# Attention of a four-layer network: moments, preparation and settling of a block cut into smaller parts, one part to a round

## The chip, the cores and the metric

The kernel runs on one core of a Trainium2 chip. The metric is the device time of one execution in microseconds (us), as the median of several runs. The engines are named as the profile names them: PE is TensorE (PEld its weight loads), DVE is VectorE, ACT is ScalarE, POOL is GpSimd, SP is SyncE.

## What is computed

The reference has four layers: a deformable convolution, a gated state-space layer, an attention by products of cosines with a feed-forward network and a mixture of experts, and last an additive attention with a second mixture of experts. The change touches the additive attention alone. For each of 4 images, with 4096 tokens of 128 channels, it computes, in float32:

```
v     = layernorm(t)                                    # over the 128 channels
s_ij  = w2 . tanh(v_i W1[:128] + v_j W1[128:] + b1) + b2   # for j before i
out_i = sum_{j<i} exp(s_ij) v_j / (sum_{j<i} exp(s_ij) + tiny)
t     = t + out
```

(The output is a softmax over the earlier tokens; 16 hidden units stand between the two matrices.)

## The kernel before

**What replaces tanh.** With the exponentials F = exp(2 f_i) and G = exp(2 g_j) of the two projections, exp(s_ij) can be written with a few sums of products F x G, their logarithm, and an exponential. The 16 hidden units are folded into three sets of products over 32 or 64 rows. For a tile of 128 keys j and 512 queries i, PE forms three denominators (D, three banks of PSUM) and three numerators (num1, num2); ACT takes Ln of D and Exp of its negative; DVE multiplies by the numerators; POOL adds the three terms to one sum q; and in a later round ACT takes Exp of the negative of q, which gives the weights e. PE then multiplies v by e and adds into acc.

**Blocks and rounds.** A block is one image n and 512 queries, ib = 0 to 7. Its keys are taken 128 at a time, so block ib has 4 ib + 3 rounds (3, 7, 11, ... 31; the last two rounds hold the pieces at the diagonal); 136 rounds an image, 544 in all. `blocks` (L2123) lists them. One round is one call of `step` (L2268), and the order in which `step` issues things is the order on every engine: the class InOrder keeps program order, and each engine works through its queue in that order. In one call, `products` (L2132) issues

- on PE the denominators of this round and the numerators of the round two calls before;
- on ACT one Ln over this round's D (r<-D), one Exp (r<-r) over that and over the q of an earlier round (2048 columns in one instruction when both are whole);
- on DVE two multiplications by numerators (r<-r,num, 1024 and 512 columns), on POOL two additions (r<-r);
- on DVE, for pieces on the diagonal, a multiplication by a triangular mask (r<-r,keep, L2213) right after this round's Exp. It comes four calls after the round whose piece it is, so it falls into rounds 1, 2 and 3 of the next block.

After that, `step` runs the functions of `later`, each holding what it got for one call: first one that only delays, then `weigh` (L2219; acc += v e on PE, and at a block's end the copy aT<-acc on DVE), then `settle` (L2232): four transposes of aT on PE into bank 3 of D, the copy zs<-D, the reciprocal den, a row sum zl, and four additions onto X, all in one call. `LAG = 4 + len(later)` is the number of empty calls at the end, and of the calls after which a block's tiles are free.

**Preparation of the next block.** While a block runs, its successor is prepared by the generator `prepare` (L2088), a part at each `next(ahead)` at the end of `step`. The parts: 0, for an even q, `statistics` (L2070), the moments of eight tiles for two blocks (eight bn_stats, six small DVE instructions, then Ln and Exp of rstd on ACT), and nothing for an odd q; 1, the norm (four v<-X,mean,rstd); 2, four transposes on PE and the copy vT<-D; 3 to 6, one product each with wf or wg (D<-vT) and its exponential on ACT, F, F, G, G, with a maximum on DVE (top) and for G a scaling on POOL in the part after; 7, the last of these. The parts are spread evenly over the block's rounds (`to`, L2290), in block 7 from round 11 on.

**Bank 3.** D has four banks. A round takes banks 0 to 2 (side 0) or 1 to 3 (side 1), so that two rounds can alternate. What `aux()` (L2024) returns, for transposes and the wf and wg products, is bank 3. Therefore a round in which bank 3 is taken, and the round after it, have side 0:

```
taken = held[-1] is not None or any(p in ON_BANK for p in parts)
side = int(last[0] == 0 and not taken and not last[1])
again = side == last[0]
```

`again` says that a round has the same side as the one before, so its denominators have to wait for that round's Ln; then `products` issues the numerators ahead of the denominators on PE, and otherwise the first denominator ahead.

Of the kernel before, what the change touches and what calls it, by code (L numbers as in the profile page):

```python
# [16 lines left out]
P = 128  # L17
# [3 lines left out]
NT = L // P  # L21
# [67 lines left out]
class Kernel:  # L89
# [1903 lines left out]
    def attention(self):  # L1993
# [10 lines left out]
        tc, nc = self.tc, self.nc  # L2004
        T = self.X.rearrange("p (t c) -> p t c", c=P)
        LAST = P - 1
        LIMIT = 4.0e8
        with ExitStack() as outer:
# [7 lines left out]
            with ExitStack() as ctx:  # L2016
# [7 lines left out]
                def aux():  # L2024
                    return D[:, 3, :]
# [24 lines left out]
                def aside(op):  # L2050
                    held_to(op, some(logs[1]) + uses, some(logs[2]))
# [15 lines left out]
                nc = InOrder(tc)  # L2067
                pieces, norm = {}, [None]

                def statistics(t0):  # L2070

                    st = sp.tile([P, 8, 6], F32, name="st")
                    mean = sp.tile([P, 8], F32, name="mean")
                    rstd = sp.tile([P, 8], F32, name="rstd")
                    d = sp.tile([P, 8], F32, name="d")
                    for k in range(8):
                        nc.vector.bn_stats(st[:, k, :], T[:, t0 + k, :])
                    nc.vector.tensor_add(mean, st[:, :, 1], st[:, :, 4])
                    nc.vector.tensor_scalar(mean, mean, 0.5, None, ALU.mult)
                    nc.vector.tensor_sub(d, st[:, :, 1], st[:, :, 4])  # L2080
                    nc.vector.tensor_mul(d, d, d)
                    nc.vector.tensor_add(rstd, st[:, :, 2], st[:, :, 5])
                    nc.vector.scalar_tensor_tensor(rstd, d, 32.0, rstd, ALU.mult, ALU.add)
                    nc.scalar.activation(rstd, rstd, AF.Ln, bias=self.eps5, scale=1.0 / P)
                    nc.scalar.activation(rstd, rstd, AF.Exp, scale=-0.5)
                    norm[0] = mean, rstd

                def prepare(n, q):  # L2088

                    v = vs[q]  # L2090
                    if q % 2 == 0:
                        statistics(n * NT + 4 * q)
                    yield
                    mean, rstd = norm[0]
                    for k in range(4):
                        t = n * NT + 4 * q + k
                        nc.vector.tensor_scalar(v[:, k, 0:LAST], T[:, t, 0:LAST], mean[:, t % 8:t % 8 + 1],
                                                rstd[:, t % 8:t % 8 + 1], ALU.subtract, ALU.mult)
                    yield
                    pd = aux()  # L2100
                    for k in range(4):
                        aside(nc.tensor.transpose(pd[:, k * P:(k + 1) * P], v[:, k, :], self.ident))
                    vT = rp.tile([P, 512], F32, name="vT", bufs=1)
                    uses[:] = [nc.vector.tensor_copy(vT, pd)]
                    wrote[0] = None
                    yield
                    out = {"v": v, "F": [], "G": []}
                    for k, (to, m) in enumerate((("F", wf[0]), ("F", wf[1]), ("G", wg[0]), ("G", wg[1]))):
                        ps = aux()
                        aside(nc.tensor.matmul(ps, m, vT, start=True, stop=True))  # L2110
                        t = bp.tile([P, 512], F32, name=f"{to}{k % 2}" + (f"_{q}" if to == "G" else ""),
                                    bufs=1 if to == "G" else 3)
                        uses[:] = [nc.scalar.activation(t, ps, AF.Exp, scale=2.0)]
                        wrote[0] = t
                        out[to].append(t)
                        yield
                        nc.vector.tensor_reduce(top[:, 8 * n + q, k:k + 1], t, AX.X, ALU.max)
                        if to == "G":
                            nc.gpsimd.tensor_scalar(t, t, cw[k % 2], None, ALU.mult)
                    pieces[n, q] = out  # L2120
                    yield

                def blocks(ib):  # L2123


                    for jt in range(4 * ib + 1):
                        yield [(jt, slice(0, 512), slice(0, 512))]
                    yield [(4 * ib + 1, slice(128, 512), slice(0, 384)),
                           (4 * ib + 3, slice(384, 512), slice(384, 512))]
                    yield [(4 * ib + 2, slice(256, 512), slice(256, 512))]  # L2130
# [101 lines left out]
                def settle(n, ib, aT):  # L2232

                    z = aux()
                    for s in range(4):
                        aside(nc.tensor.transpose(z[:, s * P:(s + 1) * P], aT[:, s * P:(s + 1) * P], self.ident))
                    zs = ep.tile([P, 512], F32, name="zs", bufs=1)
                    uses[:] = [nc.vector.tensor_copy(zs, z)]
                    wrote[0] = None
                    z = zs.rearrange("p (s c) -> p s c", c=P)  # L2240
                    den = sm.tile([P, 4], F32, name="den")
                    nc.vector.tensor_scalar(den, z[:, :, LAST], tiny, None, ALU.add)
                    nc.vector.reciprocal(den, den)
                    zl = sm.tile([P, 4], F32, name="zl")
                    nc.vector.tensor_reduce(zl, z[:, :, 0:LAST], AX.X, ALU.add)
                    nc.vector.tensor_mul(zl, zl, den)
                    t0 = n * NT + 4 * ib
                    for s in range(4):
                        tt = T[:, t0 + s, 0:LAST]
                        nc.vector.scalar_tensor_tensor(tt, z[:, s, 0:LAST], den[:, s:s + 1], tt, ALU.mult, ALU.add)  # L2250
                    tl = T[:, t0:t0 + 4, LAST]
                    nc.vector.tensor_sub(tl, tl, zl)
# [2 lines left out]


                order = [(n, q) for n in range(NB) for q in range(8)]
                for _ in prepare(*order[0]):
                    pass
                later = [lambda *a: a, weigh, settle]  # L2260
                LAG = 4 + len(later)
                waiting, sums = [None, None], [None, None]
                spaces = [rp.tile([P, 4, 512], F32, name="r", bufs=RB) for k in range(2)]
                held = [None] * len(later)
                PARTS, ON_BANK = 8, (2, 3, 4, 5, 6)
                last = [0, False]

                def step(block, parts=()):  # L2268


                    taken = held[-1] is not None or any(p in ON_BANK for p in parts)
                    side = int(last[0] == 0 and not taken and not last[1])
                    again = side == last[0]
                    last[:] = side, taken
                    new_held, new_sum, new = products(block, side, again, waiting.pop(), sums.pop())
                    waiting.insert(0, new_held)
                    sums.insert(0, new_sum)
                    for k in range(len(later)):
                        new, held[k] = (later[k](*held[k]) if held[k] is not None else None), new
                    for _ in parts:  # L2280
                        next(ahead)

                for k, (n, ib) in enumerate(order):
                    ahead, done = (prepare(*order[k + 1]), 0) if k + 1 < len(order) else (None, PARTS)
                    todo = list(blocks(ib))
                    rounds = len(todo)

                    first = 4 + LAG if ib == 7 else 0
                    for r, parts in enumerate(todo):
                        to = -(-PARTS * max(r - first + 1, 0) // (rounds - first))  # L2290
                        step((n, ib, parts, r == rounds - 1), range(done, max(done, to)))
                        done = max(done, to)
                for k in range(LAG):
                    step(None)
                nc = self.nc
# [200 lines left out]
```

## Time and profile before

| | |
|---|---|
| median of 3 runs | 5611.95 us (5593.98 to 5615.91) |
| the profiled execution | 5601.23 us, its span 5599.5 us |
| mean granted PE clock | 0.941 |
| busy over the span | PE 4991.9 (89%), DVE 4016.3 (72%), ACT 3113.9 (56%), POOL 3073.1 (55%) |
| the attention | 3077 to 5218 us of the span, 2141 us |
| r<-D (Ln) of the attention | 544, one a round; 1.44 us over 1536 columns |
| r<-r (Exp) over 2048 columns | 1.91 us |
| moments, settling | 16 and 32 times |
| F and G exponentials | 128, 0.58 us each |

How to read it: the page gives the shares over the whole span, and the attention is only 2141 us of it. Nearly every instruction of the attention is recorded under one line, L82, the helper that keeps the program order; so instructions are found by engine and by the tiles that they write and read (r<-D is one that reads D and writes r). In a timeline the columns are the start and the length in us, engine, line, operation, tiles, shapes and count, and in brackets the idle time ahead of it on its engine and who ended it.

### The profile page before, as it was taken

Reading aid. Unit: us, or ns where it says so; the run is one execution under the profiler, and the core shown is the slowest. Engines: PE = TensorE matmul, PEld = TensorE weight load, DVE = VectorE, ACT = ScalarE, POOL = GpSimd, SP = SyncE. Lnnn points to the kernel's source line nnn. Section 1 sums busy time; section 2 is a strip of 40 time slices with the busy share of each in tenths; the row PEclk is TensorE's granted clock in tenths of the full one; section 3 lists DMA queues with packets and bytes.
Section 4 is the critical chain, followed back from the end, with each engine's and each line's share of the span. In section 5 each row is a group of like instructions: output and inputs, shape, how many; then the busy total and the mean of one; then the engine's idle time right before and its main releaser. Section 6 shows DMA issues by size and latency. Waiting matters only on the chain. (4 is left out here: it accounts for less than half of the span.)

```text
span 5599.5 us, 62830 instructions
## 1 busy us (share of the span) xinstructions
PE 4991.9 (89%) x21718; PEld 2404.9 (43%) x21718; DVE 4016.3 (72%) x7854; ACT 3113.9 (56%) x3785; POOL 3073.1 (55%) x3027
## 2 busy tenths in 40 slices
PE   6898989879999859999887899989998998999887
PEld 3454444335656523333443344434433444344443
DVE  6888988758876578786698565666566666665796
ACT  1122222146655345555431689878978987889431
POOL 0525253314444324454399577666766776667597
PEclk8999999989988779999899899999999999999899
DMA  5545454400000020000000000000000000000001
GB/s 171 126 131 128 124 132 127 98 6 1 16 16 12 27 61 1 1 1 1 6 31 16 16 1 1 1 1 1 1 1 1 1 1 1 1 1 1 5 1 61
DMA packets 66743, 185.21 MB, mean 33 GB/s; under 512 B 13158, under 2 KB 16038, under 8 KB 64744
## 3 DMA queue, kind: packets, MB, share of 16 engines
q1 hardware_dynamic: 55792, 163.68, 9.9%
q0 software_dynamic: 6272, 12.86, 1.4%
q10 hardware_dynamic: 4344, 4.50, 0.3%
q8 instruction: 175, 2.87, 0.2%
q14 instruction: 160, 1.31, 0.1%
HBM read 131.63 MB, written 49.36 MB: 32 GB/s over the span
## 5 line engine op out<-in xcount | busy, mean ns | idle before, releaser
L82 POOL TENSOR_TENSOR r<-r 128x512 f32<-128x512 f32 (+1 forms) x1088 | 1349.0, 1241 | 661.9 <-DVE r L82 597.0
L82 DVE TENSOR_TENSOR r<-r,num 128x1024 f32<-128x1024 f32 (+1 forms) x1088 | 970.4, 927 | 564.3 <-PE num L82 514.1
L82 PE MATMUL D<-F,G 32*128 32x512 f32 (+3 forms) x4608 | 1218.8, 589 | 1.9 <-POOL G L82 1.0
L82 PE MATMUL num<-F,G 32*128 32x512 f32 (+3 forms) x4608 | 1084.5, 604 | 105.4 <-DVE r L82 101.6
L82 ACT ACTIVATE r<-r 128x2048 f32<-128x2048 f32 (+4 forms) x610 | 1018.3, 1679 | 49.2 <-POOL r L82 3.4
L82 ACT ACTIVATE r<-D 128x1536 f32<-128x1536 f32 (+1 forms) x544 | 764.2, 1405 | 206.1 <-PE D L82 174.2
L82 PE MATMUL acc<-pr,ident 128*128 128x512 f32 x1600 | 749.4, 619 | 79.4 <-DVE pr L82 79.4
L82 PEld LDWEIGHTS D<-F,G 32*128 32x128 f32 x4608 | 507.2, 189 | 327.4 <-issue 217.2
L82 PE MATMUL acc<-r,v 128*128 128x512 f32 (+3 forms) x1152 | 606.4, 614 | 3.1 <-DVE aT L82 3.1
L82 PEld LDWEIGHTS num<-F,G 32*128 32x128 f32 x4608 | 394.4, 187 | 410.9 <-DVE r L82 239.5
L1886 PE MATMUL pex<-w_expert_w,vT 128*128 128x512 f32 x1024 | 489.5, 618 | 78.9 <-DVE x L1889 78.8
L1896 POOL TENSOR_TENSOR x<-x 128x512 f32<-128x512 f32 (+2 forms) x576 | 472.6, 820 | 103.3 <-DVE x L1889 73.3
L82 PEld LDWEIGHTS acc<-pr,ident 128*128 128x128 f32 x1600 | 309.9, 198 | 439.4 <-issue 340.2
L82 DVE TENSOR_TENSOR pr<-v,wt 128x2560 f32<-128x2560 f32 x160 | 452.7, 2835 | 30.3 <-PE acc L82 24.6
L82 PE MATMUL pff<-hid,w_ffn_w2T 128*128 128x512 f32 x1024 | 468.4, 600 | 0.0
L82 POOL DMA_INDIRECT px<-tab,idx x196 | 330.7, 1687 | 231.5 <-DVE idx L82 159.8
L82 POOL TENSOR_TENSOR X<-X,sl 128x512 f32<-128x512 f32 x32 | 87.9, 2746 | 491.5 <-ACT sl L82 491.5
L1889 DVE TENSOR_TENSOR x<-pex,gate 128x1024 f32<-128x1024 f32 x256 | 309.1, 1213 | 62.8 <-POOL X L1897 51.1
L82 PEld LDWEIGHTS acc<-r,v 128*128 128x128 f32 x1152 | 176.7, 190 | 393.1 <-issue 263.9
L1886 PEld LDWEIGHTS pex<-w_expert_w,vT 128*128 128x128 f32 x1024 | 184.0, 193 | 329.0 <-DVE x L1889 176.9
L82 ACT ACTIVATE hid<-phh,cols 128x512 f32<-128x512 f32 x320 | 198.9, 685 | 224.2 <-PE phh L82 224.2
L82 POOL TENSOR_TENSOR Y<-y,tm 128x64 f32<-128x64 f32 x256 | 115.9, 473 | 331.1 <-DVE w L82 164.3
(563 smaller groups left out, 7379.4 us busy)
## 6 DMA issues: line engine op xcount, KB each, us to landing
v<-tab SPq DMA_DIRECT2D x320, 256.0 KB
oms<-omw SPq DMA_DIRECT2D x32, 432.0 KB
omr<-oms SPq DMA_DIRECT2D x32, 432.0 KB
X<-in_x_dram SPq DMA_DIRECT2D x8, 1024.0 KB
tab<-vb SPq DMA_DIRECT2D x64, 128.0 KB
o<-o SPq DMA_DIRECT2D x32, 256.0 KB
oin<-o SPq DMA_DIRECT2D x32, 256.0 KB
kept<-X SPq DMA_DIRECT2D x4, 2048.0 KB
```

The lines of the kernel that those rows point to most:

```text
L82: return lambda *args, **kwargs: self.tc.keep_in_program_order(op(*args, **kwargs))
L1886: nc.tensor.matmul(pex[:, 4 * h:4 * h + 4, :], vT[:, k, :], ew[:, 512 * h:512 * (h + 1)], start=True, stop=True)
L1889: nc.vector.tensor_tensor(x, pex, gate[:, k, :].unsqueeze(2).to_broadcast([P, NE, P]), ALU.mult)
L1896: nc.gpsimd.tensor_tensor(x[:, 0:w, :], x[:, 0:w, :], x[:, w:2 * w, :], ALU.add)
```

## The change

`statistics` becomes a generator with three parts: four bn_stats, the other four, and the small instructions with Ln and Exp of rstd. `prepare` runs them as parts -3, -2 and -1 when q is even; for an odd q the empty part is gone. So there are 10 or 7 parts, and bank 3 is used by parts 1 to 5. `settle` ends with the copy zs; `ratio` (den and zl) and `onto` (additions to X) follow in the next two calls, so that LAG is 9 and not 7, and block 7 begins to prepare in round 13 and not in 11. The parts are dealt out by another formula: each round takes the remaining parts over the remaining rounds, rounded up. Where a block has more rounds than parts, that is one part in each round from its first on, until all are done.

```diff
                 def statistics(t0):
                     st = sp.tile([P, 8, 6], F32, name="st")
+                    for h in range(2):
+                        for k in range(4 * h, 4 * h + 4):
+                            nc.vector.bn_stats(st[:, k, :], T[:, t0 + k, :])
+                        yield
...
-                    for k in range(8):
-                        nc.vector.bn_stats(st[:, k, :], T[:, t0 + k, :])
...
                     norm[0] = mean, rstd
+                    yield
...
                     if q % 2 == 0:
-                        statistics(n * NT + 4 * q)
-                    yield
+                        yield from statistics(n * NT + 4 * q)
...
                     wrote[0] = None
-                    z = zs.rearrange("p (s c) -> p s c", c=P)
+                    return n, ib, zs.rearrange("p (s c) -> p s c", c=P)
+
+                def ratio(n, ib, z):
                     den = sm.tile([P, 4], F32, name="den")
...
                     nc.vector.tensor_mul(zl, zl, den)
+                    return n, ib, z, den, zl
+
+                def onto(n, ib, z, den, zl):
                     t0 = n * NT + 4 * ib
...
-                later = [lambda *a: a, weigh, settle]
+                later = [lambda *a: a, weigh, settle, ratio, onto]
+                SETTLES = 2
...
-                PARTS, ON_BANK = 8, (2, 3, 4, 5, 6)
...
-                    taken = held[-1] is not None or any(p in ON_BANK for p in parts)
+                    taken = held[SETTLES] is not None or any(1 <= p <= 5 for p in parts)
...
-                    ahead, done = (prepare(*order[k + 1]), 0) if k + 1 < len(order) else (None, PARTS)
+                    ahead = done = None
+                    if k + 1 < len(order):
+                        ahead, done = prepare(*order[k + 1]), 0 if order[k + 1][1] % 2 else -3
...
-                        to = -(-PARTS * max(r - first + 1, 0) // (rounds - first))
-                        step((n, ib, parts, r == rounds - 1), range(done, max(done, to)))
-                        done = max(done, to)
+                        now = ()
+                        if ahead is not None and r >= first:
+                            now = range(done, done - (done - PARTS) // (rounds - r))
+                            done = now.stop
+                        step((n, ib, parts, r == rounds - 1), now)
```

More of the change, by code (lines that the diff above doesn't have):

```diff
@@ L2257, in attention @@
                 order = [(n, q) for n in range(NB) for q in range(8)]
+                PARTS = 7
                 for _ in prepare(*order[0]):
                     pass
-                later = [lambda *a: a, weigh, settle]
+                later = [lambda *a: a, weigh, settle, ratio, onto]
+                SETTLES = 2
                 LAG = 4 + len(later)
```

## Prediction

> **What bounds the kernel now.** I read the page first, then the windows over the attention (the change touches nothing else), then ScalarE's timeline there, and VectorE's and TensorE's where a round was longer than its neighbours.
>
> ```profile
> 3612.00:4150.00 538.00, 500.24 (x2782) 221.12 (x2777) 338.79 (x525) 463.51 (x335) 368.59 (x294) 0.97 0.00 1
> 4150.00:4680.00 530.00, 493.53 (x2697) 215.04 (x2698) 333.55 (x520) 454.16 (x326) 359.41 (x288) 0.97 0.00 1
> ```
>
> Columns: window, length, busy PE, PEld, DVE, ACT, POOL, PE clock, DMA. PE (93%) and ACT (86%) look alike full; the timeline tells which paces.
>
> ```profile
> 4430.60 1.43 ACT L82 ACTIVATE r<-D 128x1536 f32<-128x1536 f32 x1
> 4432.13 1.91 ACT L82 ACTIVATE r<-r 128x2048 f32<-128x2048 f32 x1
> 4433.94 0.58 ACT L82 ACTIVATE F<-D 128x512 f32<-128x512 f32 x1
> 4434.42 1.44 ACT L82 ACTIVATE r<-D 128x1536 f32<-128x1536 f32 x1
> ...
> 4407.97 1.45 ACT L82 ACTIVATE r<-D 128x1536 f32<-128x1536 f32 x1
> ...
> 4411.57 1.46 ACT L82 ACTIVATE r<-D 128x1536 f32<-128x1536 f32 x1
> ...
> 4415.17 1.45 ACT L82 ACTIVATE r<-D 128x1536 f32<-128x1536 f32 x1
> ...
> 4420.06 1.46 ACT L82 ACTIVATE r<-D 128x1536 f32<-128x1536 f32 x1 [1.44 <-PE D L82]
> ```
>
> Each round has one r<-D (Ln), so the distance of two of them is a round's price. The timeline knows few prices: 3.34 us for a plain round (Ln and Exp back to back: ACT paces), 3.82 after a round with an F or G exponential (4434.42 - 4430.60: its 0.48 stands on ACT), 3.60 for a round that must reuse the same side of D (4411.57 - 4407.97: `again`, ACT idles 0.25 for PE). Other rounds are stalls. All stalls together: ACT's busy time taken from the blocks' lengths leaves 280 us idle in the attention's 2141, 8.8 a block. More than that the change cannot return.
>
> Where a stall comes from is seen on VectorE, after the settling at 4413:
>
> ```profile
> 4413.06 0.69 DVE L82 COPY zs<-D 128x512 f32<-128x512 f32 x1 [0.86 <-ACT r L82]
> 4413.78 0.29 DVE L82 TENSOR_SCALAR den<-zs,tiny 128x4 f32<-128x4 f32 x1
> ...
> 4414.97 1.13 DVE L82 SCALAR_TENSOR_TENSOR X<-zs,den,X 128x127 f32<-128x127 f32 x4
> ...
> 4416.08 1.81 DVE L82 TENSOR_TENSOR r<-r,num 128x1024 f32<-128x1024 f32 x2
> ```
>
> A plain round costs VectorE 1.82 us (the two r<-r,num) and leaves it 1.32 waiting for PE. Settling is 3.0 us in one piece, so the next r<-r,num is late, PE's num waits (1.84 idle in front of it), and the Ln at 4420.06 comes 4.89 after its predecessor.
>
> **The change, part by part.** *Settling in three rounds* (copy 0.69; ratio, 4413.78 to 4414.97, 1.2; adding onto X, 1.2): each fits into 1.32. Today the two rounds behind a settle exceed their prices by 1.3 (block 5), 1.9 (block 7) and 1.6 (block 2), 40 us over the 24 settles of blocks 2 to 7. New cover: in blocks 2 to 6 the parts of preparation now run in the same rounds, so top (0.68) stands beside ratio: 1.82 + 0.68 + 1.2 = 3.7 in a round of 3.84. That just fits; I keep 0.3 to 0.4 a block as a rest (bounds 0 and 1.5). If the cover is gone, the old 1.5 comes back.
>
> *Parts in successive rounds instead of spread.* The new range takes one part a round from a block's start (from round 13 in block 7), the old one spread eight over all rounds. A round that uses bank 3 forces side 0 on itself and the next. Five in a row force six rounds, five apart up to ten. Following `step` through the code gives 241 repeated rounds of 544 before and 180 after; those that follow no F or G exponential (where ACT covers the repeat) fall from 124 to 58. 66 x 0.25 = 16 us (contained in the block sums below). The 128 exponentials stay, at 0.48, but in blocks 2, 4 and 6 move from plain rounds into rounds 3 to 6, where ACT idles anyway. Their price there is zero to 0.48; it is inside the windows below. PE's transposes and the wf and wg products stay behind their round's products, as now, and no DMA moves. On POOL, scaling G (1.56 by the groups by form) now falls into two successive rounds: 2.62 + 1.56 against 3.83 leaves it 0.35 late twice; the sum q that it delays is read by Exp two rounds later, so I cost it at nothing (without that cover 0.7 a block, 20 in all).
>
> *Moments in three rounds.*
>
> ```profile
> ACT rstd L82 <- DVE rstd L82: 95.8, 13, 75.5
> ...
> 4386.46 1.64 DVE L82 BATCH_NORM_STATS2 st<-X 128x6 f32<-128x128 f32 x8
> 4388.13 0.54 DVE L82 TENSOR_TENSOR mean<-st 128x8 f32<-128x8 f32 x1
> ```
>
> Of 95.8 us in the waits, 75.5 is one wait before the attention's loop; only 20 can be won. Half the bn_stats is 0.82 and the small chain 1.25 (4388.13 to 4389.38): each fits into 1.32. But the chain's place moves. In blocks 3 and 5 it now falls into round 2, which is a *mask round*: the diagonal's r<-r,keep (rounds 1 to 3, the last three rounds of the block before, four rounds on) waits on VectorE for this round's Exp:
>
> ```profile
> 4396.72 1.19 DVE L82 TENSOR_TENSOR r<-r,keep 128x128 f32<-128x128 f32 x2 [1.32 <-ACT r L82]
> 4397.84 1.10 DVE L82 TENSOR_SCALAR v<-X,mean,rstd 128x127 f32<-128x127 f32 x4
> 4398.86 1.81 DVE L82 TENSOR_TENSOR r<-r,num 128x1024 f32<-128x1024 f32 x2
> ```
>
> So a new wait: Ln of rstd, and behind it on ACT the next round's Ln and Exp, wait for Exp, keep (0.9), chain (1.25), then rstd 0.45: 2.6 us, all on the path. The mask rounds are the heart of the risk. Undisturbed (block 7) they cost 4.28, 4.24, 4.04; with a VectorE step beside the mask, one becomes 6.8:
>
> ```profile
> 4489.22 1.23 PE L82 MATMUL num<-F,G 32*128 32x512 f32 x3 [0.95 <-DVE r L82]
> 4490.23 1.07 PE L82 MATMUL num<-F,G 32*128 32x512 f32 x3
> ...
> 4398.00:4406.00 8.00, 6.84 (x29) 2.61 (x31) 5.36 (x9) 4.31 (x5) 4.23 (x4) 0.79 0.00 0
> ```
>
> Matmuls of 0.59 take 1.06 to 1.23 and the granted clock is 0.79 after a PE gap of only 0.95. The Trainium skill ("TensorE: Matmul & The Clock Gate", HAM oscillation) rules that idle gaps over about 3.4 us throttle the array. By it, no gap of these windows (2 to 3 us) would, and a num-to-Ln stretch is 2.1 us (4417.95 to 4420.06); by the rows it is 3.65 (4400.72 to 4404.37). I take the row once per window in blocks 3 and 5, half of it in 2, 4 and 6. The same skill's overview ("Trainium Architecture — The Big Picture", What this means for kernel authors) calls the port that VectorE and GpSimd share an exclusive lock: by it the four v of the norm wait for POOL's additions. The timeline has both, 1.10 here and 2.78 at 4620.22. Moving norm into round 3 keeps that lottery; I take the middle.
>
> *By block*, first Ln to the next block's, mean of the images, 3.9 being a repeated round with 0.3 of the settle's rest, "window" being Ln of round 2 to Ln of round 6:
> - Blocks 4 and 6: norm moves out of the mask rounds to round 0, vT and top move in. Exp, keep and vT (1.0), r<-r,num (1.82), PE (2.1) give Ln of round 3 at 4.9 after round 2's; round 4's at 8.3; round 5's waits for keep and top of round 3, at 13.2 warm or 14.7 cold; plus 3.84: 17 to 18.5, I take 17.75 (now 18.4 and 18.9). Block 6: 3.6 x 2 + 17.75 + 3.9 + 19 x 3.35 + 2.45 = 95.0, now 98.7. Block 4: 11 in place of 19: 68.0, now 70.3.
> - Block 2: 3.9 + 3.6 + 17.75 + 3.9 + 3 x 3.35 + 2.8 = 42.0, now 45.9.
> - Blocks 3 and 5: window 18.4 to 21.5 by the new wait and norm after keep, I take 20 (now 18.3). Block 5: 3.4 + 3.34 + 20 + 11.9 + 13 x 3.35 + 2.25 = 84.4, now 85.5. Block 3: 58.1, now 59.2.
> - Block 7: mask rounds as now (22.6 to round 6), 3.6, ten plain 33.5, rstd 0.45 and norm's stall of 0.86 as now, 3.6, four at 3.83, eight plain 26.8, 2.35: 109.1, now 112.2.
> - Block 1 (7 rounds): now 36.4; in the first image, where no settle falls into its mask round, 32.1. I take 32. Block 0: 20.4, one part less in a round: 19.4.
>
> Sum: 3.7 + 2.3 + 3.9 + 1.1 + 1.1 + 3.1 + 4.4 + 1.0 = 20.6 an image, 82 in all. The two extra calls of `step` at the end issue nothing but the last settle. The profiled execution (5601.2, span 5599.5) stands 11 under the median of 5612; 82 off the median gives 5530.
>
> **Rivals.**
> - *The settle isn't hidden*: top, ratio and G's scaling meet in blocks 2 to 6 and VectorE runs late as before; 3.7 of 3.84 speaks for it, the plain rounds' slack against. Then 20 x 1.5 to 2 comes back, 35: 5565.
> - *Mask rounds eat it*: windows 3 us longer each than I put them, 20 x 3 = 60: 5590, no change.
> - *Slower*: in blocks 2 to 6 every mask round now carries a VectorE step and a repeated side, PE gaps grow past 2 us, and the clock stays down for two rounds of a window (1.5 each) with norm at 2.8 and the rstd wait on top; window 25 in place of about 18.6. 20 x 6.4 = 128 against 82: 5658. Outside the windows the gain is 23.4 an image, so it turns where a window passes 23. Today no block over block 1 has more than one such cold round in these four, which speaks against it.
>
> **Chances.** Forecast 0.55, settle not hidden 0.20, eaten 0.14, slower 0.11. 0.5% (28 us) is about what a measurement here can tell from no change; the first two lie beyond it, but for a slip: faster 0.74, same 0.15, slower 0.11. Low end: windows at block 7's bare 15.9 in blocks 2, 4 and 6 and no rest at settles, 35 lower, 5495; the high end takes in the eaten case, 5595.
>
> **What would show it.** After the change: 4.9 and 5.2 gone behind settles; long runs of 3.34 in the second half of blocks 3 to 6 and 3.83 only in four successive rounds; a wait of ACT rstd on DVE of some 2.6 in blocks 3 and 5, and a long round 4 or 5 there with PE at half speed. If windows in blocks 2 to 6 pass 23, or 4.9 stays behind settles, I am wrong.

## The result, and the profile after

Over 22 runs each the median is 5602.2 us before and 5589.4 us after; the ratio is 0.9982 (95% interval 0.9974 to 0.9990). The change saves 10 to 13 us where 82 were forecast. The profiled spans say the same: 5599.5 and 5587.7 us.

The windows over the attention (same columns as in the prediction) of the changed kernel:

```profile
3600.00:4138.00 538.00, 504.88 (x2794) 217.34 (x2788) 356.68 (x527) 465.74 (x336) 370.98 (x296) 0.97 0.00 1
4138.00:4668.00 530.00, 495.38 (x2744) 215.17 (x2740) 352.28 (x523) 457.88 (x331) 364.50 (x290) 0.98 0.00 1
```

PE, ACT and POOL did what they did before. VectorE is busy 18 us longer in each window with nearly the same number of instructions (527 for 525, 523 for 520): some of them have become longer. That is the first sign of what went wrong.

Blocks, from the block's first Ln to the next block's, mean of the four images (block 7 of the three that another image follows), in us, and the change beside the forecast:

| block | before | after | change | forecast |
|---|---|---|---|---|
| 0 | 20.4 | 21.3 | +0.9 | -1.0 |
| 1 | 36.4 | 39.3 | +2.9 | -4.4 |
| 2 | 45.9 | 43.8 | -2.1 | -3.9 |
| 3 | 59.2 | 60.1 | +0.9 | -1.1 |
| 4 | 70.3 | 68.3 | -2.0 | -2.3 |
| 5 | 85.5 | 86.5 | +1.0 | -1.1 |
| 6 | 98.7 | 95.1 | -3.6 | -3.7 |
| 7 | 112.2 | 110.3 | -1.9 | -3.1 |

That is 3.9 us an image and not 20.6. Of the 16.7 us that are missing, 9.2 are missing in blocks 0 and 1. Blocks 4 and 6 came out as forecast, but by luck: a new stall of 1.1 us stands in them too, and the window from round 2 to round 6 is 1.2 us shorter than it was put. Three kinds of stall are left.

*A stall two calls after onto.* ACT's timeline in block 6, rounds 8 to 10:

```profile
4498.66 1.43 ACT L82 ACTIVATE r<-D 128x1536 f32<-128x1536 f32 x1
...
4502.00 1.43 ACT L82 ACTIVATE r<-D 128x1536 f32<-128x1536 f32 x1
...
4506.43 1.45 ACT L82 ACTIVATE r<-D 128x1536 f32<-128x1536 f32 x1 [0.99 <-PE D L82]
```

The round of 4.9 right behind the settle is gone, but the Ln at 4506.43 comes 4.43 after its predecessor instead of 3.34. VectorE at that place:

```profile
4497.82 1.80 DVE L82 TENSOR_TENSOR r<-r,num 128x1024 f32<-128x1024 f32 x2
4499.55 2.95 DVE L82 SCALAR_TENSOR_TENSOR X<-zs,den,X 128x127 f32<-128x127 f32 x4
4502.41 0.16 DVE L82 TENSOR_TENSOR X<-X,zl 128x4 f32<-128x4 f32 x1
4502.49 1.81 DVE L82 TENSOR_TENSOR r<-r,num 128x1024 f32<-128x1024 f32 x2
```

The four additions (onto) take 2.95 us; in the kernel before they took 1.13. The view of the tile zs, first of the kernel before, then of the changed one (minimum, median and maximum of one instruction in ns):

```profile
L82 DVE SCALAR_TENSOR_TENSOR X<-zs,den,X x128: 339/345/350, 3149.8 to 5217.1; 128x127 f32<-128x127 f32 x128
```

```profile
L82 DVE SCALAR_TENSOR_TENSOR X<-zs,den,X x128: 336/341/1447, 3161.0 to 5204.8; 128x127 f32<-128x127 f32 x128
```

The median is the same, the longest is four times as long. Summed over all 128 it is 44 us before and 90 after. What the long ones wait for is seen when the first two of the four are laid beside POOL's two additions, each in a window of its own (4499.7 to 4500.5 and 4500.7 to 4501.8):

```profile
4499.55 1.07 DVE L82 SCALAR_TENSOR_TENSOR X<-zs,den,X 128x127 f32<-128x127 f32 x1
4499.19 1.28 POOL L82 TENSOR_TENSOR r<-r 128x512 f32<-128x512 f32 x1
4500.54 1.43 DVE L82 SCALAR_TENSOR_TENSOR X<-zs,den,X 128x127 f32<-128x127 f32 x1
4500.54 1.28 POOL L82 TENSOR_TENSOR r<-r 128x512 f32<-128x512 f32 x1
```

Each ends 0.15 us after the POOL instruction beside it (4500.62 after 4500.47, 4501.97 after 4501.82). So do all other long ones: 51 of the 128 take over 0.5 us, and each of these ends 0.14 to 0.15 us after the POOL instruction beside it. In the kernel before none is that long: POOL was idle beside 124 of the 128 and all but done beside the other four. At the settle in block 5:

```profile
4411.42 2.63 POOL L82 TENSOR_TENSOR r<-r 128x512 f32<-128x512 f32 x2 [0.96 <-ACT r L82]
4417.44 2.62 POOL L82 TENSOR_TENSOR r<-r 128x512 f32<-128x512 f32 x2 [3.39 <-DVE r L82]
```

The settle's four additions stood between the two, from 4414.97 on.

*The wait for rstd.* ACT in block 5, between round 2 and round 3:

```profile
4389.34 1.91 ACT L82 ACTIVATE r<-r 128x2048 f32<-128x2048 f32 x1
4393.85 0.30 ACT L82 ACTIVATE rstd<-rstd,eps 128x8 f32<-128x8 f32 x1 [2.60 <-DVE rstd L82]
...
4394.30 1.43 ACT L82 ACTIVATE r<-D 128x1536 f32<-128x1536 f32 x1
```

This is the wait that the prediction put at 2.6 us. In blocks 3 and 5 the Ln of round 3 now comes 6.48 to 6.85 us after that of round 2.

*PE behind a copy.* PE in block 1 (first fence) and block 5 (second):

```profile
4177.92 1.09 PE L82 MATMUL D<-ident,v 128*128 128x128 f32 x4 [0.48 <-DVE v L82]
4182.77 2.08 PE L82 MATMUL D<-vT,wf 128*128 128x512 f32 x2 [3.76 <-DVE vT L82]
4184.78 1.23 PE L82 MATMUL num<-F,G 32*128 32x512 f32 x3
```

```profile
4408.85 1.13 PE L82 MATMUL D<-vT,wf 128*128 128x512 f32 x2 [1.08 <-DVE zs L82]
```

In block 1 the transposes of v and the product with wf stand in one round. PE has to wait 3.76 us for the copy vT, which on VectorE stands behind the mask's r<-r,keep and aT; the next round's num stands behind the product in PE's queue, and the row of three takes 1.23 where the same row otherwise takes 0.70. In block 5 the product waits for zs of the settle that falls into the same round, and the next Ln comes 5.39 us after its predecessor.

### The profile page after: what moved, and what is told of

Its sections match the earlier page's. It is cut to its first block, busy times and chain, and to the rows that moved or that the text cites. A ratio compares the mean times of both kernels' runs of the same rounds, so it can differ in the third digit from the quotient of the medians.

```text
span 5587.7 us, 62851 instructions
## 1 busy us (share of the span) xinstructions
PE 5003.7 (90%) x21718; PEld 2403.7 (43%) x21718; DVE 4078.7 (73%) x7854; ACT 3109.8 (56%) x3785; POOL 3079.8 (55%) x3027
## 5 line engine op out<-in xcount | busy, mean ns | idle before, releaser
L82 PE MATMUL D<-F,G 32*128 32x512 f32 (+3 forms) x4608 | 1239.0, 587 | 1.0 <-POOL G L82 1.0
```

The source lines that it names most:

```text
L82: return lambda *args, **kwargs: self.tc.keep_in_program_order(op(*args, **kwargs))
```

## The experiments

Theory after the result: three separate causes, onto lengthened by POOL's additions, the parts of blocks 0 and 1, and the moments' chain in a mask round. Rival: the prediction's own, that the mask rounds with parts eat the gain. Ratios are to the kernel before, run beside each; a difference from the changed kernel is one of two ratios, so it is known to some 10 us only. "The attention" is the time from its first Ln to its last Exp in the one profiled execution of each kernel (2099.8 us in the changed one).

**One part of the change alone: settling in three calls.** On the kernel before:

```diff
-                later = [lambda *a: a, weigh, settle]
-                LAG = 4 + len(later)
+                later = [lambda *a: a, weigh, settle, ratio, onto]
+                LAG = 7
```

> The kernel before with one part of the change alone: settling in three calls (copy, ratio, onto); moments and the dealing of parts as before. Theory (the step's price was taken where POOL stood still; beside POOL's additions the small VectorE instructions are longer: the 128 scalar_tensor_tensor of onto took 44 us in all before and 90 us after the change): each settle still makes a later round 1 us late, so only 5 to 15 us of the 40 come back, ratio 0.997 to 0.999. Rival (the settle is hidden as the prediction says and the gain is eaten in the mask rounds): 30 us or more come back, ratio 0.995 or less.

Measured: 0.9991 (0.9980 to 1.0001), 5 us, and the interval holds 1. Onto is long here too (its additions sum to 89 us), and block 7 has the round of 4.40 two calls after onto, where block 7 before had its 5.21. The theory held in its cause and nearly in its number; splitting alone gives back little or nothing.

**The dealing of the parts alone.** On the changed kernel, settle and moments in one piece again:

```diff
-                later = [lambda *a: a, weigh, settle, ratio, onto]
+                later = [lambda *a: a, weigh, settle]
...
-                        ahead, done = prepare(*order[k + 1]), 0 if order[k + 1][1] % 2 else -3
+                        ahead, done = prepare(*order[k + 1]), 0 if order[k + 1][1] % 2 else -1
```

> The changed kernel with settling and moments in one piece each again, so that only the dealing of the parts (one a round from the block's start) is left of the change. Theory: blocks 4 and 6 gain some 2 us each by fewer repeated rounds, blocks 0 and 1 lose 4 us an image, blocks 3 and 5 lose by the moments near the mask rounds and a product beside a settle: ratio 0.999 to 1.002. Rival (mask rounds eat the change): windows of blocks 2 to 6 over 20 us, ratio over 1.004.

Measured: 1.0051 (1.0038 to 1.0065), 28 us longer than the kernel before: the rival's number, but not its cause. The windows of the mask rounds are 16.4 to 17.3 us and not over 20. In blocks 2, 4 and 6 the long round is the one two calls after the settle, 7.5 to 8.2 us but once. VectorE in block 6:

```profile
4512.22 0.69 DVE L82 COPY zs<-D 128x512 f32<-128x512 f32 x1 [1.00 <-ACT r L82]
4512.95 1.19 DVE L82 TENSOR_SCALAR den<-zs,tiny 128x4 f32<-128x4 f32 x1
...
4516.15 0.68 DVE L82 TENSOR_REDUCE top<-G 128x1 f32<-128x512 f32 x1
4516.75 1.81 DVE L82 TENSOR_TENSOR r<-r,num 128x1024 f32<-128x1024 f32 x2
```

In these blocks the last part of the preparation falls into round 6, where the settle is; with den lengthened to 1.19 that makes 4.5 us ahead of the next r<-r,num. PE then stands idle for 2.29 us (at 4518.61), and its next matmuls take 1.06 in place of 0.59. So the dealing needs the split settle: the split is worth 5 us at most with the old dealing and (1.0051 to 0.9947, the run with moments whole below) 58 with the new.

But not in every block. From this run to the one with moments whole, which differ by the split alone (and by block 7's start), blocks 2, 4 and 6 fall by 8.1, 3.5 and 3.6 us, while blocks 3 and 5 grow by 2.0 and 1.9. Against the theory, which had them lose, blocks 3 and 5 are here 2.6 and 2.3 us shorter than before the change. In block 5 the whole settle falls into the time for which PE is late anyway with a product behind zs, and POOL is idle (PE's row at 4430.13 has 1.08 us of waiting for zs):

```profile
4431.48 1.13 DVE L82 SCALAR_TENSOR_TENSOR X<-zs,den,X 128x127 f32<-128x127 f32 x4
4433.45 1.56 POOL L82 TENSOR_SCALAR G<-G,cw 128x512 f32<-128x512 f32 x1 [2.89 <-DVE top L82]
```

Whole in blocks 3 and 5 and split in the others would by these numbers be some 16 us less (an estimate: 3.9 us over four images); no run tries it.

**Blocks 0 and 1 in the old groups.** On the changed kernel:

```diff
+                            if ib < 2:
+                                now = range(done, ((2, 5, 7), (1, 2, 3, 4, 5, 6, 7))[ib][r])
```

> The changed kernel with the parts of blocks 0 and 1 in the same groups as before the change (norm and vT; F, F, G; G and the rest in block 0; moments and norm in block 1's first round, then one a round). Theory: blocks 0 and 1 grew by 0.9 and 2.9 us an image because a product with wf stands on PE right behind a copy of vT of the same round and PE waits for it (3.8 us once an image); with the old groups 12 to 20 us go, ratio to the kernel before 0.994 to 0.996. Rival (the split settle or moments make these blocks longer): under 5 us go, ratio 0.9975 or more.

Measured: 0.9951 (0.9935 to 0.9968), 17 us less than the changed kernel by the ratios, 19 by ACT's idle time in the attention (260.5 us for 279.2). Theory held: it is the grouping that made these blocks longer, not the split settle. But block 1 is then 36.5 us, as it was before the change, and not the 32 of the forecast. From the second image on, a settle falls into its round 3, and PE waits 3.01 us for its zs in both kernels (at 4193.19 before, at 4173.24 here); what round 3 loses otherwise (8.7 us and more before, 7.4 to 8.3 here), the last round gains (3.03 before, 5.03 here).

**Without most of onto.** Three of four additions onto X are left out:

```diff
                     for s in range(4):
                         tt = T[:, t0 + s, 0:LAST]
-                        nc.vector.scalar_tensor_tensor(tt, z[:, s, 0:LAST], den[:, s:s + 1], tt, ALU.mult, ALU.add)
+                        if s == 0:
+                            nc.vector.scalar_tensor_tensor(tt, z[:, s, 0:LAST], den[:, s:s + 1], tt, ALU.mult, ALU.add)
```

> The changed kernel, leaving out three of the four additions onto X in every settle (X then lacks most of the attention). Theory (onto, 2.9 us beside POOL, doesn't fit into the 1.32 us that a round leaves): the rounds of 4.4 and 5.1 us two calls after onto become 3.34 to 3.6 in blocks 2 to 7, 25 to 35 us go against the changed kernel, ratio to the kernel before 0.992 to 0.994. Rival (these long rounds come from ratio, top or G's scaling): under 10 us go, ratio over 0.9965.

Measured: 0.9897 (0.9883 to 0.9912), 48 us less than the changed kernel, more than expected; ACT's idle time falls by 41. This takes out the additions' own work (0.34 us each) together with their wait. Block 6, rounds 9 and 10:

```profile
4469.56 1.43 ACT L82 ACTIVATE r<-D 128x1536 f32<-128x1536 f32 x1
...
4472.90 1.43 ACT L82 ACTIVATE r<-D 128x1536 f32<-128x1536 f32 x1
```

3.34 where the changed kernel had 4.43. Of the single causes tried, onto is worth the most.

**Onto with one input in PSUM.** For the settles that fall into blocks 4, 6 and 7, ratio and onto read z in bank 3, and zs isn't made:

```diff
+                    if ib in (3, 5, 6):
+                        return n, ib, z.rearrange("p (s c) -> p s c", c=P)
...
-                    taken = held[SETTLES] is not None or any(1 <= p <= 5 for p in parts)
+                    taken = held[2] is not None or any(h is not None and h[1] in (3, 5, 6) for h in held[3:]) or any(1 <= p <= 5 for p in parts)
```

> The changed kernel; in the settles that fall into blocks 4, 6 and 7 (12 of 32) ratio and onto read z from bank 3 of PSUM, without the copy zs, and the bank stays taken two rounds longer. Theory (onto waits for POOL because it has two inputs in SBUF, a port it shares with POOL): with one input in PSUM the four additions take 1.2 to 1.6 us in these settles and not 2.9, the rounds of 4.4 there fall to 3.6 or less, two more repeated rounds cost 0.5; net 4 to 10 us less than the changed kernel, ratio to the kernel before 0.9965 to 0.9975. Rival (the additions are slow by X itself or by their own chain): they stay at 2.9 and the repeats make it 6 us longer, ratio 0.999 to 1.0.

Measured: 1.0005 (0.9994 to 1.0017). The cause is as the theory has it, the time as the rival has it. VectorE and POOL, then PE, in block 6:

```profile
4498.26 1.12 DVE L82 SCALAR_TENSOR_TENSOR X<-D,den,X 128x127 f32<-128x127 f32 x4 [0.85 <-ACT r L82]
4494.21 5.32 POOL L82 TENSOR_TENSOR r<-r 128x512 f32<-128x512 f32 x4
```

```profile
4499.27 0.66 PE L82 MATMUL D<-F,G 32*128 32x512 f32 x1 [0.49 <-DVE X L82]
```

Beside POOL the four additions take 1.12 again, and none of the 48 with an input in PSUM is long. But ratio and onto, reading D, now each wait for a Ln, as the copy zs alone did, and PE waits for onto, so the Ln of round 9 comes 4.56 after that of round 8; by the ratios the kernel is 13 us longer than the changed one. Whether these waits are the program's or the chip's was not tested.

**Parts of blocks 3 to 6 later**, and from block 3 on no part in a round that settles.

```diff
-                    first = 4 + LAG if ib == 7 else 0
+                    first = (0, 0, 0, 4, 9, 9, 9, 4 + LAG)[ib]
...
-                        if ahead is not None and r >= first:
+                        if ahead is not None and r >= first and not (ib > 2 and held[SETTLES] is not None):
```

> The changed kernel with the parts of blocks 3 to 6 dealt later: block 3 from round 4 on, blocks 4 to 6 from round 9 on, and no part in a round that settles. Theory: the wait of ACT for the moments' chain in round 2 of blocks 3 and 5 (2.6 us), the product that PE holds behind zs in round 6 (1.5) and top beside onto (0.5) go: 2 to 4 us a block in blocks 3 and 5; blocks 4 and 6 lose 1 to 2 since F and G exponentials move out of the mask rounds where ACT idles: in all 0 to 15 us less than the changed kernel, ratio to the kernel before 0.9955 to 0.9985. Rival (the mask rounds with parts are what keeps the change from its gain): blocks 4 and 6 gain as well, 25 us or more, ratio under 0.994.

Measured: 0.9971 (0.9963 to 0.9980). That is 6 us less than the changed kernel, but the two intervals overlap and the attention is as long as there (2099.5 us), so a gain is not shown. Block 5 falls by 2.7 us as expected, block 3 by 0.7 only, and blocks 4 and 6 grow by 2.3 and 1.5. The rival, my own of the prediction, falls: in blocks 4 and 6 the mask rounds are the better place for parts.

**Moments in one part**, the first diff of the change undone and -1 in place of -3.

> The changed kernel with the moments in one part (all eight bn_stats, chain, Ln and Exp of rstd in one round, two rounds earlier than the chain stands in the changed kernel, so out of the mask round in blocks 3 and 5). Theory: splitting moments brought nothing; in blocks 3 and 5 the whole part in round 0 costs 1.0 us in the next round and the 2.6 us wait goes: 0 to 12 us less than the changed kernel, ratio to the kernel before 0.996 to 0.9985. Rival (splitting is what the change gains by): 10 us or more longer than the changed kernel, ratio 1.0 or more.

Measured: 0.9947 (0.9930 to 0.9964), 20 us less than the changed kernel by the ratios, 12 by the profiled spans, 17 by the attention: more than the theory had. The wait of ACT for rstd in block 5 is

```profile
4375.11 0.30 ACT L82 ACTIVATE rstd<-rstd,eps 128x8 f32<-128x8 f32 x1 [0.46 <-DVE rstd L82]
```

Splitting the moments is a loss. In blocks 3 and 5, which fall by 1.6 and 1.4 us, the split had moved the chain two rounds on, to the mask. The rest of the gain stands in blocks 0 and 1 (0.4 and 1.0); its cause stays open.

**Onto in two calls**, two additions each; then **onto in two instructions**:

```diff
-                    for s in range(4):
+                    for s in (2 * half, 2 * half + 1):
```

> The changed kernel with onto in two successive calls, two additions each (zs in two buffers, LAG 10). Theory (beside POOL's additions onto takes 2.9 us where a round leaves VectorE 1.32; in halves of some 1.5 with r<-r,num's 1.82 it is 3.3): the rounds of 4.4 two calls after onto fall to 3.4 to 3.7 and those of 5.1 in blocks 3 and 5 to about 4: 15 to 28 us less than the changed kernel, ratio to the kernel before 0.9932 to 0.9956. Rival (each half waits for POOL afresh, so that the sum grows): under 8 us less, ratio over 0.9968.

```diff
-                        nc.vector.scalar_tensor_tensor(tt, z[:, s, 0:LAST], den[:, s:s + 1], tt, ALU.mult, ALU.add)
+                    nc.vector.tensor_tensor(zz, zz, den.unsqueeze(2).to_broadcast([P, 4, LAST]), ALU.mult)
+                    nc.vector.tensor_tensor(tt, tt, zz, ALU.add)
```

> The changed kernel with the four scalar_tensor_tensor of onto replaced by two tensor_tensor over 508 columns (zs times den, then X plus zs). Theory, after the halves: each VectorE instruction with two inputs in SBUF waits for POOL's running addition (up to 1.27 us), so the count of instructions is what costs; two of them take 2.0 to 2.6 us and not 2.95, the rounds of 4.4 fall to 3.7 to 4.1: 5 to 15 us less than the changed kernel, ratio to the kernel before 0.9955 to 0.9975. Rival (the bytes moved beside POOL set the time): 2.9 us or more, no better than the changed kernel, ratio 0.998 or more.

Measured: 1.0004 (0.9990 to 1.0018) and 1.0004 (0.9991 to 1.0016): both misses, both 12 us longer than the changed kernel (15 by the attention). VectorE in block 6 with the halves:

```profile
4499.67 2.41 DVE L82 SCALAR_TENSOR_TENSOR X<-zs,den,X 128x127 f32<-128x127 f32 x2
4502.00 1.81 DVE L82 TENSOR_TENSOR r<-r,num 128x1024 f32<-128x1024 f32 x2
4503.73 2.33 DVE L82 SCALAR_TENSOR_TENSOR X<-zs,den,X 128x127 f32<-128x127 f32 x2
```

and with two instructions:

```profile
4508.58 1.46 DVE L82 TENSOR_TENSOR zs<-zs,den 128x508 f32<-128x508 f32 x1
4510.07 1.65 DVE L82 TENSOR_TENSOR X<-X,zs 128x508 f32<-128x508 f32 x1
```

The three forms fit one account: alone the instructions would take 1.13 (four), about 0.65 (two, 0.34 each) and about 1.36 (0.675 and 0.687 at the least in that run); beside POOL they take 2.95, 2.41 and 3.1, so 1.75 to 1.8 more in every call. POOL has two additions in a round, and onto is held up once by each. So neither count nor size helps, and every further call pays afresh. The rows bear this out one by one: with the halves 105 of the 128 additions take over 0.5 us, and each ends 0.14 to 0.15 us after the POOL instruction beside it; and where the run without most of onto kept one addition, it took 1.05 in block 6, held up once.

**Several together.** Onto in two calls, moments whole and the old groups in blocks 0 and 1 (the run e9):

> The changed kernel with three things together: onto in two calls, moments in one part, and the old groups of parts in blocks 0 and 1. Theory (three separate causes): the gains add, 17 + 15 + 20 = 52 us less than the changed kernel, ratio to the kernel before 0.987 to 0.991. Rival (they are one stall seen three times): no better than the best of them alone, ratio 0.9935 or more.

Measured: 0.9940 (0.9918 to 0.9962), hardly better than the old groups or whole moments alone, as the rival has it. The same with block 5 from round 9 on and block 3 without a part in the settle's round (e10):

> The kernel of e9 with block 5's parts from round 9 on, and block 3's product out of the round that settles. Theory (PE holds a product with wf behind the copy zs of the same round, 1.5 us a block): 4 to 12 us less than e9. Rival (the parts cost the same wherever they stand): within 3 us of e9.

Measured: 0.9920 (0.9895 to 0.9945), median 5550.1, the lowest of the kernels that leave nothing out; its interval overlaps that of e9. Of its two parts one worked: block 3 falls by 3.4 us against e9, block 5 grows by 0.7. And onto in one call, moments whole, old groups, no part in the settle's round in blocks 3 and 5 (e12):

> The changed kernel with the old groups of parts in blocks 0 and 1, moments in one part, and no part in the round that settles in blocks 3 and 5; onto as in the changed kernel, in one call. Theory (three separate causes, and onto in halves was a loss in e9 and e10): 19 + 17 + 15 to 20 us less than the changed kernel, ratio to the kernel before 0.988 to 0.991. Rival (the causes overlap): ratio 0.993 or more.

Measured: 0.9935 (0.9918 to 0.9952). The sums for e9 and e12 were set too high. In e12 blocks 0 and 1 give back their 19 us, but in block 3 (third image) the distance of two Ln after round 6 falls from 5.39 to 3.59 while the one after round 9 rises from 5.08 to 5.48, where onto takes 3.23 in place of 2.92: removed in one place, a stall comes back in part in another, so the gains don't add. What is left to the 0.985 forecast is probably onto's, but no run takes onto out together with the other two causes, and no form of onto was found that waits neither for POOL nor for something else.

## Why the prediction was wrong

- *The step that failed* is "Settling in three rounds (... adding onto X, 1.2): each fits into 1.32". The 1.2 was read where the settle stood in one piece. There the r<-r,num was late, and POOL, which waits for it, idle for 3.39 us. Split, onto runs beside POOL's additions and takes 2.95. That leaves a round of 4.4 in blocks 2, 4, 6 and 7 and of 5.1 in blocks 3 and 5, where 3.35 and a rest of 0.3 to 0.4 a block were booked. Leaving three quarters of it out, work and wait together, is worth 48 us. The prediction named the shared port, and used it for the norm alone.
- *Blocks 0 and 1* were not worked out but set ("I take 32"). They carry up to three and two parts in a round, and PE's queue stops behind a copy. They are missed by 9.2 us an image, 37 us of the 67 that the blocks' sums miss in all. The old groups bring back half. The other half was never won: with them block 1 is as long as before the change, and PE waits in it for zs as before (3.01).
- *Moments.* The new wait was seen, and its size right (2.60). What was wrong was to book blocks 3 and 5 as a gain after it: moments whole take 12 to 20 us less over all blocks. A piece that fits into a round's slack needn't be cut, and where it stands matters more.
- *A product beside a settle in blocks 3 and 5* (5.39 after round 6, 1.5 above its price) wasn't seen: PE's transposes and products were booked as standing "behind their round's products, as now".
- *What was right*: a round's prices of 3.34, 3.6 and 3.83, the long runs of 3.34, the 4.9 and 5.2 behind settles gone. The windows of blocks 2, 4 and 6 are 16.5 to 16.6 (17.75 forecast), those of 3 and 5 18.9 to 19.0 (20), so the two rivals built on them fall. That they came out shorter than forecast is what hid onto's stall in blocks 4 and 6. (The windows called "now" in the prediction are those of the third image; over the four images they were 17.5 and 18.0 in blocks 4 and 6, and 17.7 and 18.0 in 3 and 5.) The half-speed clock was still met in blocks 3 and 5, as the row said and the rule didn't: 1.06 in place of 0.59 after a gap of 1.59 us (4390.78 us of the changed kernel), with a granted clock of 0.79 from 4388 to 4396.
- By its number (5590) the rival "mask rounds eat it" is nearest to the 5589.4 measured, but by chance, since the windows came out shorter than forecast and not 3 us longer. By its place nearest was "the settle isn't hidden" (5565), with another cause than it named.

## What to carry to other kernels

A duration is a price only together with what ran beside it: before a step is moved next to another engine's work, look up whether that engine was idle where the duration was read. Cut a step up where the pieces land in real slack, leave it whole where it falls into time that another engine takes anyway, and check for each piece what stands behind it in every queue; a copy between two PE instructions of one round stops PE for all that follows. A dealing rule that is right for long blocks can be wrong for the shortest, and these have to be worked out one by one.

## What the runs showed of the hardware

Small VectorE instructions with both inputs in SBUF, and the one-input tensor_scalar (den, 0.22 alone, up to 0.93 in the changed kernel; v, 0.34 and up to 1.43), lengthen beside POOL's additions (beside POOL's scaling of G, which has one input, den stayed at 0.22); the mask's r<-r,keep, with two inputs in SBUF, does so too (25 of 128 over 0.5 us in the changed kernel, each ending 0.15 after POOL's instruction). Those that read PSUM (X<-D,den,X at 1.12 for four, the copies at 0.69), the maxima (0.67) and bn_stats (0.28) do not. The Trainium skill's "GPSIMD Engine Reference" (Specifications) names contention with GpSimd for VectorE's instructions in a 2-port mode or with two SBUF inputs, and gives no time there. The rows agree for two inputs; whether tensor_scalar ran in such a mode no run here shows. The time here is what is left of each POOL instruction met: 1.75 to 1.8 us for a call of onto that meets two, about 0.7 for the single addition that meets one. The profile counts that wait as busy time of VectorE, so no row of waits shows it.
